# A graph network's opening: x ahead of the convolution taps, in block order, planned, with zero matmuls ahead of it

## The chip, the cores and the metric

The kernel runs on one NeuronCore of a Trainium2 chip. Five engines work at once and are tied by semaphores: TensorE (PE, matmuls into PSUM), VectorE (DVE), ScalarE (ACT), GpSimd (POOL) and SyncE (SP), which here only issues DMA transfers. The metric is the time on the device in microseconds (us), the median of several executions.

## The reference

Input: `x` of shape (64, 256, 256), that is 64 graphs of 256 nodes with 256 channels, and an adjacency matrix of 256 x 256 for each graph. One layer is computed, all in float32:

```
h     = relu(layernorm(x))                    # no learned scale
c     = relu(bn1(conv1(h)))                   # conv of width 1 over the nodes, 256 to 256 channels
x_conv= relu(bn2(conv2(c)) + h)               # conv of 17 taps over the nodes, 256 to 256 channels
s     = h @ w_se.T + b_se                     # 3 numbers for each node
A     = exp(-|s_n - s_m|^2) * adj
x_nmp = A @ relu(h @ w_msg.T + b_msg)
out   = x + GRU(input=[x_conv, x_nmp], state=h)   # sigmoid r and z, tanh n
```

## The kernel before

**Tiling.** The graphs are taken in pairs (`G = 2`, 32 pairs), and eight graphs (four pairs, `PB = 4`) make a block; there are eight blocks. The convolution of 17 taps is done in a transformed domain: the nodes of a graph are seen as `(b h c)` with 16 blocks b, 8 positions h and 2 halves c, so that 16 nodes make a block of length `L = 16`; additions on VectorE (`split`, then `forward` with an odd and an even part) transform the blocks, TensorE multiplies each of 16 frequencies by its filter (`begin`, `complete`), and `branch_back` and the like transform back.

**Filters.** The transformed filters are made once, in the opening. `filter_steps` calls `filters` 57 times (19 groups of input channels by three passes over the frequencies): two matmuls of the taps by fixed points, a copy from PSUM by ScalarE into one of the buffers `evicted`, and a DMA write of that buffer to a DRAM tensor `filt`. From there `load_kinds` brings filters back into nine slots `wb`, 256 KB each, for the products.

**The opening.** Loads are issued first (from `nc.first = 0` to `nc.first = None`, line 685 on), in this order for each queue: the vectors of the second batch norm by GpSimd; fixed points, half of the first taps, the vectors of the first batch norm, the conv1 weights and the other taps by ScalarE; and by SyncE the other half of the first taps, x of pair 0, more taps, x of pair 1, more taps, x of pairs 2 and 3. Then for each pair of the first block: `norm` (statistics on VectorE, a power of -1/2 on GpSimd, scaling on VectorE), `transpose_h` (eight transposes by TensorE into PSUM, evicted with the relu into `HT`), `conv1` (matmuls; evicted with scale, shift and relu into `h1`) and `split`. Evictions of pair 0 are done by VectorE, the others by ScalarE. Filter steps are put between the pairs. After that come `forward(0)`, which needs pairs 0 and 1, `forward(1)`, which needs pairs 2 and 3, the remaining filter steps, and `message`, `embed` and `affinity` of pair 0.

**Rows of x.** `rows` gives the DMA side of a graph as `(b h c) d -> h b (c d)`: the partition is h x 16 + b, and each holds two rows, 2 KB, in a row. `transpose_h` can then write `HT` in the order of PSUM, which is the order `(c, h, b)` that the rest of the kernel uses.

**The order of the work.** No instruction is issued at once: `Recorder` keeps every operation with the operations it depends on, and `emit` writes them out. `plan` is a list scheduler: it has a cost for each operation, and for a DMA a size in us (from the bytes, the length of runs and `share`, a number of parallel parts) and one common clock `self.dma`; at each step it takes the engine that can start first and on it the operation whose due time `late` (counted back from TensorE's program order) is least. Operations recorded while `nc.first` is a number keep their order ahead of all others. With `emit(True)` the order is that of the code, and only the times are kept. The kernel has three such parts: the four pairs of the opening with `emit(True)`, `forward` up to the last filter step with `emit()`, and the main loop over the eight blocks with `emit()`.

All operations are recorded through one helper line, so the profile shows line L370 nearly everywhere, and the names of tiles tell the work apart: `aux` and `acc` are PSUM buffers, `fo` the filter evictions, `x`, `T`, `Sv`, `PT` the places of pairs 0 to 3 (the last three are unused halves of other buffers), `st`, `mv`, `rstd` the statistics, `U`, `V`, `Sv`, `T`, `PT` the transforms.

Of the kernel before, what the change touches and what calls it, by code (L numbers as in the profile page):

```python
# [13 lines left out]
FP = mybir.dt.float32  # L14
U16 = mybir.dt.uint16
AF = mybir.ActivationFunctionType
ALU = mybir.AluOpType
# [232 lines left out]
class Recorder:  # L250
# [14 lines left out]

    def __init__(self, nc):
        self.nc, self.tasks, self.live, self.masks = nc, [], {}, {}
        self.first, self.planned, self.dma = None, 0, 3.0
        self.lanes = [deque([0.0] * self.LANES) for _ in range(2)]
        self.free = dict.fromkeys(self.LAG, 0.0)  # L270
        for name in ("tensor", "vector", "scalar", "gpsimd", "sync"):
            setattr(self, name, Proxy(self, name))
# [60 lines left out]
    def record(self, engine, op, args, kw):  # L333
        method = getattr(getattr(self.nc, engine), op)
        out = kw["out"] if "out" in kw else args[0]
        ins = [v for v in list(args) + list(kw.values()) if isinstance(v, bass.AP) and v is not out]
        n = 1
        for s in out.shape[1:]:
            n *= s
        size = 0  # L340
        if op.startswith("dma"):
            if "transpose" in op:
                size, cost = 2.5, self.TURN
            elif "accum_op" in kw:
                size, cost = 2.3, 1.0
            else:
                k = 10 if engine == "gpsimd" else self.share(out, ins[0])
                run = min(self.run(v) for v in (out, ins[0]))
                size = n * out.shape[0] * WIDTH[out.dtype] * 16 / k / 330e3 * max(1, 1400 / run)
                cost = 0.35 if k > 10 and run > 1024 else 0.62  # L350
        elif engine == "tensor":
            cost = n / 597 + 0.006
            if op == "transpose":
                cost = out.shape[-1] / 1170
            elif args[1].shape[0] < 32:
                cost = 0.23
        elif engine == "vector":
            cost = {"bn_stats": 0.33, "bn_aggr": 0.07}.get(op, n / 960 + 0.07)
            if op == "tensor_mul" and n == 256:
                cost = 0.5  # L360
        elif engine == "scalar":
            cost = n / 1400 + (0.2 if op == "activation" else 0.12)
            if out.dtype == U16:
                cost = n / 860
            elif len(out.shape) == 3 and op == "activation" and n == 256:
                cost = 0.49
        else:
            cost = 1.1 if self.planned == 0 else 7.0 if ALU.pow in args else 2.0
        k = len(self.tasks)
        self.tasks.append(Task(engine, lambda: method(*args, **kw), cost, size, self.first))  # L370
        if self.first is not None:
            self.first += 1
        for v in ins:
            self.access(k, v, False)
        self.access(k, out, True)
        return k
# [106 lines left out]
def kernel(  # L483
# [19 lines left out]
    P = 128  # L503
# [33 lines left out]
    def keep(name, *dims):  # L537
        return const.tile([P, *dims], FP, name=name)
# [24 lines left out]
    st, mv, rstd, shift = (Ring(keep(f"{name}{k}", *dims) for k in range(2)) for name, dims in (  # L563
        ("st", (G * MC, 6)), ("mv", (G * MC, 2)), ("rstd", (G * MC,)), ("shift", (G * MC,))))
    SLOTS = 9
    slots = [keep(f"wb{k}", DC, D) for k in range(SLOTS)]
    aux = Ring(psum.tile([P, W], FP, name=f"aux{k}") for k in range(4))
    acc = Ring(psum.tile([P, 2, W], FP, name=f"acc{k}") for k in range(2))
# [12 lines left out]
    def rows(t, g):  # L581
        return t[g].rearrange("(b h c) d -> h b (c d)", h=L // 2, c=MC)

    def row_tile(t, g):
        return t[:, g * MC:(g + 1) * MC, :].rearrange("p c d -> p (c d)")
# [5 lines left out]
    def chunk(t, g, c):  # L591
        return t[:, g * N + c * P:g * N + (c + 1) * P]
# [2 lines left out]
    SPARE = {k + 1: t[:, SL // 4:] for k, t in enumerate((Tt, Svt, PTt))}  # L595
    X, ADJ, HT, XNM, STATS = {}, {}, {}, {}, {}

    def load_rows(t, src, i, eng):
        for g in range(G):
            eng.dma_start(out=row_tile(t, g), in_=rows(src, G * i + g))  # L600

    def load_x(i, eng=nc.sync):
        if i >= NP:
            return
        X[i] = SPARE[i].rearrange("p (q d) -> p q d", d=D) if i in SPARE else x_rows
        load_rows(X[i], x, i, eng)

# [38 lines left out]

    PASSES = [range(0, 6), range(6, 12), range(12, 16)]
    taps = stage.tile([KG * TAPS, NG, DC, D], FP, name="taps")  # L650
    evicted = Ring(stage.tile([P, W], FP, name=f"fo{k}") for k in range(6))
    bank_points = [filter_points(p, TAPS) for p in PASSES]
    points = [stage.tile([P, KG * f.shape[1]], FP, name=f"points{n}") for n, f in enumerate(bank_points)]

    def load_taps(dc, a, b, eng):
        v = c2_wT[dc * P + a * KG:dc * P + b * KG].rearrange("(g k) t o -> (k t) g o", k=KG)
        eng.dma_start(out=taps[:MAIN, a:b, dc, :], in_=v[:MAIN])
# [9 lines left out]
    def load_points(n, eng):  # L667
        f = bank_points[n]
        m = np.zeros((P, KG, f.shape[1]), np.float32)
        for k in range(KG):  # L670
            m[k * TAPS:(k + 1) * TAPS, k] = f
        eng.dma_start(out=points[n], in_=tc.nc.inline_tensor(m.reshape(P, -1), name=f"points{n}").ap())
# [4 lines left out]
    def load_vectors(name, srcs, eng):  # L677
        n = [v.shape[0] // P for v in srcs]
        t = const.tile([sum(n), P], FP, name=f"{name}_rows")
        for j, v in enumerate(srcs):  # L680
            a = sum(n[:j])
            eng.dma_start(out=t[a:a + n[j]], in_=v.rearrange("(k p) -> k p", p=P))
        ROWS[name] = t, n

    nc.first = 0
    load_vectors("bn2", bn2 + [ih_b, hh_b], nc.gpsimd)
    load_points(0, nc.scalar)
    for dc, eng in ((0, nc.sync), (1, nc.scalar)):
        load_taps(dc, *PARTS[0], eng)
        load_last_taps(dc, eng)  # L690
    load_x(0)
    load_vectors("bn1", bn1, nc.scalar)
    nc.scalar.dma_start(out=w_c1, in_=c1_wT.rearrange("(k p) o -> p k o", p=P))
    for n in range(1, len(PASSES)):
        load_points(n, nc.scalar)
    load_taps(0, *PARTS[1], nc.sync)
    load_x(1)
    load_taps(1, *PARTS[1], nc.scalar)
    load_taps(0, *PARTS[2], nc.sync)
    load_taps(1, *PARTS[2], nc.scalar)  # L700
    load_last_group(0, nc.sync)
    load_last_group(1, nc.scalar)
    load_x(2)
    load_x(3)
    nc.first = None
    nc.gpsimd.memset(Z, 0.0)
    nc.gpsimd.memset(Z[:, 0, :, 2 * SE:KD], 1.0)
# [2 lines left out]
    nc.scalar.activation(keep("unused", 1), neg_half[:, :1], AF.Relu)  # L710

    mm, transpose = nc.tensor.matmul, (lambda p, v: nc.tensor.transpose(p, v, ident))

    def columns(name):
        t, n = ROWS[name]
# [24 lines left out]
    def norm(i):  # L740
        stats(i)
        for j in range(G * MC):
            nc.vector.tensor_scalar(X[i][:, j, :], X[i][:, j, :], STATS[i][1][:, j, 0:1], STATS[i][2][:, j:j + 1],
                                    ALU.subtract, ALU.mult)
# [14 lines left out]
    def transpose_h(i):  # L759
        HT[i] = hts()  # L760
        for dc in range(DC):
            p = aux()
            for j in range(G * MC):
                transpose(chunk(p, j // MC, j % MC), X[i][:, j, dc * P:(dc + 1) * P])
            if i == 0:
                nc.vector.tensor_scalar(HT[i][:, dc, :], p, 0.0, None, ALU.max)
            else:
                nc.scalar.activation(HT[i][:, dc, :], p, AF.Relu)

# [421 lines left out]
    def filter_steps(n):  # L1193
        for _ in range(n):
            banks[0] += 1
            p = acc()[:, 0] if banks[0] % 3 == 0 else aux()
            filters(p, *steps.popleft(), nc.gpsimd if len(steps) % 2 else nc.sync)
# [1 line left out]
    norm(0)  # L1199
    bn1 = columns("bn1")  # L1200
    s1, h1_shift = fold_bn(bn1, "bn1")
    filter_steps(2)
    transpose_h(0)
    norm(1)
    for j in range(PB):
        if j > 0:
            transpose_h(j)
        if 0 < j < PB - 1:
            norm(j + 1)
        if j == 2:  # L1210
            nc.gpsimd.dma_start(out=w_msg[:, :, D:], in_=se_wT.rearrange("(k p) s -> p k s", p=P))
            for t, v in ((b_msg[:, :D], msg_b), (b_msg[:, D:], se_b)):
                nc.gpsimd.dma_start(out=t, in_=bass.AP(tensor=v.tensor, offset=v.offset, ap=[[0, P], [1, v.shape[0]]]))
            nc.sync.dma_start(out=w_msg[:, :, :D], in_=msg_wT.rearrange("(k p) o -> p k o", p=P))
            load_adj(0, nc.sync)
        conv1(j, True)
        if j == 2:
            *bn2, b_ih, b_hh = columns("bn2")
            s2, h2_shift = fold_bn(bn2, "bn2", 1.0 / L)
            b_rz = keep("b_rz", 2 * DC)  # L1220
            nc.vector.tensor_add(b_rz, b_ih[:, :2 * DC], b_hh[:, :2 * DC])
            nc.vector.tensor_scalar(b_rz, b_rz, 0.5, None, ALU.mult)
        split(j)
        filter_steps((4, 6, 2, 2)[j])
    nc.emit(True)
    load_x(PB)
    forward(0)
    forward(1)
# [201 lines left out]
```

## Time and profile before

| | |
|---|---|
| time, median of 3 | 1750.55 us (1741.92 to 1751.39) |
| span of the profiled execution | 1740.1 us |
| TensorE busy | 1667.2 us, 96% |
| VectorE busy | 1463.1 us, 84% |
| ScalarE busy | 1039.5 us, 60% |
| GpSimd busy | 245.6 us, 14% |
| DMA | 260.88 MB, mean 150 GB/s |

In the trace the opening lasts to about 110.6 us, when the last filter matmul ends and the first product of the main loop starts; it is 6% of the span. The rows of digits in the page are tenths of busy time in 40 equal slices, each 43.5 us here. A table by stretch gives, for each engine, the busy time and the number of instructions in parentheses. "MATMUL ... x8" counts machine instructions: a float32 matmul of the code appears as two of them, a transpose as one. The chain lists what was waited for, with start and length in us.

### The profile page before, as it was taken

How to read it: one execution, taken by the hardware profiler on the slowest of the kernel's cores; microseconds unless marked ns; L12 is line 12 of the kernel's file. 1: busy time of each engine (PE TensorE's matmuls, PEld its weight loads, DVE VectorE, ACT ScalarE, POOL GpSimd, SP SyncE). 2: the span in 40 equal slices, each digit the busy share in tenths (PEclk: the TensorE clock that was granted, in tenths of full speed). 3: DMA queues.
4: the chain of work that ended last, by engine and by line, in shares of the span. 5: the costliest groups of instructions: out<-in, count | busy, mean ns of one | idle time of the engine just before them, and what ended most of it. 6: DMA issues, size and time to landing. Idle time of an engine off the chain costs nothing.

```text
span 1740.1 us, 26075 instructions
## 1 busy us (share of the span) xinstructions
PE 1667.2 (96%) x8950; PEld 1414.8 (81%) x8950; DVE 1463.1 (84%) x3400; ACT 1039.5 (60%) x1949; POOL 245.6 (14%) x241
## 2 busy tenths in 40 slices
PE   5989999999999999999999999999999999999996
PEld 3768788888789888897888887898888978888885
DVE  3888998799897998788987988979988889879553
ACT  1545665576656756567655766557566666556543
POOL 2210231002210221102211031102211022100010
PEclk9999999999999999999999999999999999999998
DMA  8775365875669565684657746595656846375122
GB/s 192 224 263 176 73 140 116 244 190 105 124 130 281 118 137 112 169 244 98 127 121 231 189 98 117 127 275 122 137 106 185 234 97 126 75 234 135 22 52 49
DMA packets 326264, 260.88 MB, mean 150 GB/s; under 512 B 204616, under 2 KB 252004, under 8 KB 326131
## 3 DMA queue, kind: packets, MB, share of 16 engines
q1 hardware_dynamic: 293738, 213.72, 46.5%
q0 software_dynamic: 29440, 42.83, 12.9%
q10 hardware_dynamic: 2953, 2.66, 0.8%
q8 instruction: 70, 1.15, 0.3%
q14 instruction: 63, 0.52, 0.1%
HBM read 156.03 MB, written 43.78 MB: 115 GB/s over the span
## 4 chain that ended last, share of the span: by engine, by line
PE 84%; DVE 7%; DMA 6%; ACT 2%; issue 1%; SPq 0%; POOL 0%; ACTq 0%; DVEq 0%
PE acc L370 58%; PE aux L370 26%; DMA wb<-filt 3%; DVE V L370 2%; DVE T L370 1%; DMA x<-in_x_dram 1%; DMA hh<-halves 1%; DMA T<-in_x_dram 1%; DVE U L370 1%; DVE tr L370 1%; DVE acc L370 0%; SPq L370 0%; DVE e L370 0%; DVE gn L370 0%; ACT e L370 0%
## 5 line engine op out<-in xcount | busy, mean ns | idle before, releaser
L370 PE MATMUL acc<-wb,w_ih 128*128 128x256 f32 x768 | 192.4, 379 | 0.0
L370 POOL DMA_DIRECT2D back<-in_x_dram x62 | 63.0, 1154 | 763.3 <-ACT back L370 738.7
L370 PEld LDWEIGHTS acc<-wb,w_ih 128*128 128x128 f32 x768 | 145.9, 190 | 19.8
L370 POOL TENSOR_TENSOR rstd<-rstd,neg_half 128x4 f32<-128x4 f32 x32 | 88.6, 2768 | 418.9 <-DVE shift L370 214.7
L370 PE MATMUL acc<-wb,w_x 128*128 128x256 f32 x576 | 137.3, 382 | 8.6 <-DVE acc L370 8.6
L370 PE MATMUL aux<-wb,w_x 128*128 128x256 f32 x576 | 140.0, 381 | 3.6 <-ACT e L370 2.8
L370 DVE SCALAR_TENSOR_TENSOR V<-T,V 128x128 f32<-128x128 f32 (+2 forms) x448 | 141.1, 382 | 0.0
L370 PEld LDWEIGHTS acc<-wb,w_x 128*128 128x128 f32 x576 | 107.7, 190 | 36.3 <-DVE acc L370 16.3
L370 PEld LDWEIGHTS aux<-wb,w_x 128*128 128x128 f32 x576 | 107.7, 190 | 22.1 <-ACT e L370 5.2
L370 PE MATMUL acc<-V,wb 128*128 128x128 f32 x1024 | 118.7, 276 | 4.9 <-DMA wb<-filt 3.6
L370 PE MATMUL aux<-w_msg,hT 128*128 128x259 f32 x512 | 121.5, 382 | 0.4 <-ACT fo L370 0.4
L370 PEld LDWEIGHTS acc<-V,wb 128*128 128x128 f32 x1024 | 116.2, 192 | 6.1 <-DMA wb<-filt 4.6
L370 PEld LDWEIGHTS acc<-U,wb 128*128 128x128 f32 x1024 | 116.9, 192 | 0.9
L370 PE MATMUL acc<-U,wb 128*128 128x128 f32 x1024 | 117.1, 275 | 0.0
L370 DVE TENSOR_TENSOR T<-Yv 128x512 f32<-128x512 f32 (+1 forms) x80 | 42.5, 581 | 85.6 <-ACT Yv L370 85.1
L370 ACT COPY back<-gn 128x1024 uint16<-128x1024 uint16 x62 | 81.3, 1348 | 49.7 <-DMA gn<-back 49.7
L370 PE MATMUL aux<-hT,w_c 128*128 128x512 f32 x224 | 107.1, 596 | 3.8 <-ACT e L370 2.7
L370 PE MATMUL acc<-wb,w_hh 128*128 128x256 f32 x384 | 109.9, 381 | 0.0
L370 PE MATMUL acc<-Yv,w_ih 128*128 128x256 f32 x384 | 109.6, 381 | 0.1
L370 PEld LDWEIGHTS aux<-w_msg,hT 128*128 128x128 f32 x512 | 96.3, 190 | 15.4 <-ACT fo L370 0.8
L370 PE MATMUL acc<-hT,w_hh 128*128 128x256 f32 x384 | 105.6, 381 | 0.7 <-ACT acc L370 0.7
L370 PE MATMUL acc<-xnm,w_ih 128*128 128x256 f32 x384 | 103.9, 379 | 0.0
(176 smaller groups left out, 3841.0 us busy)
## 6 DMA issues: line engine op xcount, KB each, us to landing
wb<-filt SPq DMA_DIRECT2D x376, 256.0 KB
back<-in_x_dram POOLq DMA_DIRECT2D x62, 256.0 KB, 7.4
out_dram<-back POOLq DMA_DIRECT2D x62, 256.0 KB, 4.3
x<-in_x_dram SPq DMA_DIRECT2D x58, 256.0 KB
halves_d<-halves SPq DMA_DIRECT2D x28, 512.0 KB
adjh<-halves_d SPq DMA_DIRECT2D x112, 128.0 KB
hh<-halves SPq DMA_DIRECT2D x108, 128.0 KB
filt<-fo POOLq DMA_DIRECT2D x18, 252.0 KB, 5.1
```

Source lines behind the costliest of these rows:

```text
L370: self.tasks.append(Task(engine, lambda: method(*args, **kw), cost, size, self.first))
```

## The change

It concerns the opening only, and has five parts.

1. x of the first four pairs is loaded ahead of all taps (on SyncE's queue), and the vectors of the first batch norm move to GpSimd's queue, so that the pairs can be worked on while the taps come in.
2. These loads, and that of pair 4 (`i <= PB`), take the rows in block order: `blocks` gives `(b h c) d -> b h (c d)`, one contiguous stretch of DRAM. The node order that the rest needs is restored in `transpose_h`: the eviction reads PSUM as `(q b h)` and writes `(q h b)`.
3. `emit(True)` is gone: the opening is planned together with `forward` and the filters. The steps put between the pairs are 1, 2, 3, 3 instead of 2 and then 4, 6, 2, 2. The planner's start of the DMA clock goes from 3.0 to 2.3, and the share of a GpSimd transfer becomes the larger of 10 and what the shapes give.
4. TensorE multiplies zeros 24 times (`WARM`) into a PSUM buffer that is overwritten later, from a tile that GpSimd sets to zero first, so that it has been at work when x comes.
5. Filter evictions have 8 buffers instead of 6. The second batch norm's folding and the loads of the message weights and the first adjacency move behind the fourth pair in the code.

```diff
-        self.first, self.planned, self.dma = None, 0, 3.0
+        self.first, self.planned, self.dma = None, 0, 2.3
...
-                k = 10 if engine == "gpsimd" else self.share(out, ins[0])
+                k = max(self.share(out, ins[0]), 10 if engine == "gpsimd" else 1)
...
+    WARM = 24
...
-    def load_rows(t, src, i, eng):
+    def load_rows(t, src, i, eng, rows=rows):
...
+    def blocks(t, g):
+        return t[g].rearrange("(b h c) d -> b h (c d)", h=L // 2, c=MC)
...
-        load_rows(X[i], x, i, eng)
+        load_rows(X[i], x, i, eng, blocks if i <= PB else rows)
...
-    evicted = Ring(stage.tile([P, W], FP, name=f"fo{k}") for k in range(6))
+    evicted = Ring(stage.tile([P, W], FP, name=f"fo{k}") for k in range(8))
...
     nc.first = 0
+    nc.gpsimd.memset(e_tile[:, 0], 0.0)
+    load_vectors("bn1", bn1, nc.gpsimd)
     load_vectors("bn2", bn2 + [ih_b, hh_b], nc.gpsimd)
+    nc.scalar.dma_start(out=w_c1, in_=c1_wT.rearrange("(k p) o -> p k o", p=P))
+    for j in range(PB):
+        load_x(j)
     load_points(0, nc.scalar)
     for dc, eng in ((0, nc.sync), (1, nc.scalar)):
         load_taps(dc, *PARTS[0], eng)
         load_last_taps(dc, eng)
-    load_x(0)
-    load_vectors("bn1", bn1, nc.scalar)
-    nc.scalar.dma_start(out=w_c1, in_=c1_wT.rearrange("(k p) o -> p k o", p=P))
...
-    load_taps(0, *PARTS[1], nc.sync)
-    load_x(1)
...
-    load_x(2)
-    load_x(3)
...
+    p = aux()
+    for _ in range(WARM):
+        mm(p[:, :P], e_tile[:, 0, 0, :P], e_tile[:, 0, 0, :P], start=True, stop=True)
...
+            t = HT[i][:, dc, :].rearrange("p (q h b) -> p q h b", h=L // 2, b=NW)
+            u = p.rearrange("p (q b h) -> p q h b", h=L // 2, b=NW)
...
-                nc.vector.tensor_scalar(HT[i][:, dc, :], p, 0.0, None, ALU.max)
+                nc.vector.tensor_scalar(t, u, 0.0, None, ALU.max)
...
-    filter_steps(2)
-    transpose_h(0)
-    norm(1)
     for j in range(PB):
         if j > 0:
-            transpose_h(j)
-        if 0 < j < PB - 1:
-            norm(j + 1)
...
+            norm(j)
+        transpose_h(j)
         conv1(j, True)
...
         split(j)
-        filter_steps((4, 6, 2, 2)[j])
-    nc.emit(True)
+        filter_steps((1, 2, 3, 3)[j])
```

More of the change, by code (lines that the diff above doesn't have):

```diff
@@ L690 @@
         load_last_taps(dc, eng)
-    load_x(0)
-    load_vectors("bn1", bn1, nc.scalar)
-    nc.scalar.dma_start(out=w_c1, in_=c1_wT.rearrange("(k p) o -> p k o", p=P))
     for n in range(1, len(PASSES)):
         load_points(n, nc.scalar)
-    load_taps(0, *PARTS[1], nc.sync)
-    load_x(1)
-    load_taps(1, *PARTS[1], nc.scalar)
-    load_taps(0, *PARTS[2], nc.sync)
-    load_taps(1, *PARTS[2], nc.scalar)
+    for part in PARTS[1:]:
+        load_taps(0, *part, nc.sync)
+        load_taps(1, *part, nc.scalar)
     load_last_group(0, nc.sync)
     load_last_group(1, nc.scalar)
-    load_x(2)
-    load_x(3)
     nc.first = None
@@ L764, in transpose_h @@
                 transpose(chunk(p, j // MC, j % MC), X[i][:, j, dc * P:(dc + 1) * P])
+            t = HT[i][:, dc, :].rearrange("p (q h b) -> p q h b", h=L // 2, b=NW)
+            u = p.rearrange("p (q b h) -> p q h b", h=L // 2, b=NW)
             if i == 0:
-                nc.vector.tensor_scalar(HT[i][:, dc, :], p, 0.0, None, ALU.max)
+                nc.vector.tensor_scalar(t, u, 0.0, None, ALU.max)
             else:
-                nc.scalar.activation(HT[i][:, dc, :], p, AF.Relu)
+                nc.scalar.activation(t, u, AF.Relu)
     HP = P // 2
@@ L1201 @@
     s1, h1_shift = fold_bn(bn1, "bn1")
-    filter_steps(2)
-    transpose_h(0)
-    norm(1)
     for j in range(PB):
         if j > 0:
-            transpose_h(j)
-        if 0 < j < PB - 1:
-            norm(j + 1)
[L1210 to L1215, printed above, removed]
-        conv1(j, True)
[L1217 to L1222, printed above, removed]
-        split(j)
-        filter_steps((4, 6, 2, 2)[j])
-    nc.emit(True)
+            norm(j)
+        transpose_h(j)
+        conv1(j, True)
+        split(j)
+        filter_steps((1, 2, 3, 3)[j])
+    *bn2, b_ih, b_hh = columns("bn2")
+    s2, h2_shift = fold_bn(bn2, "bn2", 1.0 / L)
+    b_rz = keep("b_rz", 2 * DC)
+    nc.vector.tensor_add(b_rz, b_ih[:, :2 * DC], b_hh[:, :2 * DC])
+    nc.vector.tensor_scalar(b_rz, b_rz, 0.5, None, ALU.mult)
+    nc.gpsimd.dma_start(out=w_msg[:, :, D:], in_=se_wT.rearrange("(k p) s -> p k s", p=P))
+    for t, v in ((b_msg[:, :D], msg_b), (b_msg[:, D:], se_b)):
+        nc.gpsimd.dma_start(out=t, in_=bass.AP(tensor=v.tensor, offset=v.offset, ap=[[0, P], [1, v.shape[0]]]))
+    nc.sync.dma_start(out=w_msg[:, :, :D], in_=msg_wT.rearrange("(k p) o -> p k o", p=P))
+    load_adj(0, nc.sync)
     load_x(PB)
```

## The prediction

> **What bounds the kernel now.** I read first the engine rows of the page, then a table of engine time by stretch of the opening, then the chain of waits through it, and last the order of instructions on TensorE. The page:
>
> ```profile
> PE   5989999999999999999999999999999999999996
> ...
> PEclk9999999999999999999999999999999999999998
> ...
> PE 84%; DVE 7%; DMA 6%; ACT 2%; issue 1%; SPq 0%; POOL 0%; ACTq 0%; DVEq 0%
> ```
>
> TensorE is the bound: full in nearly every slice, 84% of the chain. The first slice (43.5 us) is the one with a hole. The stretches (columns: PE, PE weight load, DVE, ACT and POOL busy, PE clock, DMA share, GB/s):
>
> ```profile
> 0.00:16.00 16.00, 0.00 (x0) 0.00 (x0) 0.75 (x2) 0.00 (x0) 5.50 (x17) 1.00 0.77 143
> 16.00:40.00 24.00, 19.41 (x55) 12.11 (x56) 14.07 (x45) 5.98 (x10) 4.48 (x6) 0.86 0.93 234
> 40.00:60.00 20.00, 19.32 (x78) 12.49 (x77) 11.26 (x39) 11.02 (x19) 6.89 (x10) 1.00 0.52 163
> 60.00:80.00 20.00, 20.00 (x93) 16.52 (x92) 20.00 (x51) 11.67 (x22) 5.33 (x10) 1.00 0.81 251
> 80.00:110.60 30.60, 25.82 (x108) 16.11 (x106) 29.93 (x88) 16.59 (x42) 6.58 (x12) 0.89 0.71 218
> 110.60:140.00 29.40, 26.25 (x214) 25.27 (x214) 18.06 (x52) 8.04 (x15) 3.10 (x4) 1.00 0.93 325
> ```
>
> TensorE does nothing for 16 us, VectorE is half idle until 60, and both are then full to 110.6, where the last filter matmuls end and the products of the main loop begin. The chain says why:
>
> ```profile
> 2.48 13.67 DMA x<-in_x_dram
> ...
> 16.17 10.65 DMA T<-in_x_dram
> ...
> 113.06 8.05 PE acc L370 x72
> ...
> 121.13 10.75 DMA wb<-filt
> ```
>
> The start is two loads of x in a row: pair 0 complete at 16.2, pair 1 (into tile T) at 26.8. The DMA rate in the first of them shows that the loads are slow, not only late:
>
> ```profile
> 2.80:5.60 2.80, 0.00 (x0) 0.00 (x0) 0.00 (x0) 0.00 (x0) 2.74 (x8) 1.00 1.15 227
> 5.60:11.20 5.60, 0.00 (x0) 0.00 (x0) 0.00 (x0) 0.00 (x0) 0.70 (x1) 1.00 0.79 108
> ```
>
> 227 GB/s while the first taps move, 108 once x and the last tap rows are what is left. The same filter matmuls also differ:
>
> ```profile
> 16.28 3.93 PE L370 MATMUL aux<-taps,points 119*126 119x256 f32 x8
> 40.87 1.89 PE L370 MATMUL aux<-taps,points 119*126 119x256 f32 x8
> ```
>
> Right after the idle stretch the same eight take twice as long.
>
> [...]
>
> **The change, part by part.**
>
> *Work on TensorE.* None of the opening's real work is removed. 57 filter steps: four instructions take 0.86 us in the chain, so 49.0 us. conv1: 3.70 us per pair in the timeline, 14.8 for four. Transposes: 1.04 per pair, 4.2. Messages: 16 instructions, 0.86 per four, 3.5. Embedding, affinity, transposes of e and vectors: about 3.5. Sum 75 us, against 94.5 us from 16.1 to 110.6. So 19.5 us of that stretch are waits and slow clock, on top of 16 empty ones.
>
> *x first, in block order.* First data moved at 2.8 us. Pair 0 is 0.51 MB, and ScalarE's queue (conv1 weights, points) moves some 0.35 MB beside it: 0.86 MB at 227 GB/s is 3.8 us, so pair 0 is there at 6.6 (at 350 GB/s, the best slice of these 16 us, 5.3). I take 6.6, against 16.2. All four pairs and what runs beside them, 2.9 MB at 230 GB/s, are there by about 15.4. SyncE's half of the first taps, 0.47 MB, follows at 17.5. Filter steps thus start 1.2 us *later* than now; this is the price of the new order.
>
> *Vectors of bn1* now go by the GpSimd queue, where such loads took 9.2 to 9.9 us to land: ready at 11 to 13. The first to need them is the eviction of conv1 of pair 0, at about 15. Nothing.
>
> *TensorE until 17.5.* Norm of pair 0: statistics 1.5, aggregation 0.36, one add, the power on GpSimd about 1.2 with its hand-over, scaling 1.38: 4.5 us. Transposes start at 11. By 17.5 TensorE has done about one pair, 4.7 us of the 75.
>
> *Then.* 17.5 + 70.3 = 87.8 if it never waits. In the present trace TensorE and its weight loads still wait on ACT evictions, e and messages for about 5 us between 84 and 110; I keep 4 of them. The last filter step ends at about **92**, instead of 110.6.
>
> *VectorE.* It was busy 82.4 us from 13.9 to 117.2, of which 1.9 belong to pair 4: 80.5. From 6.6, with 5 us of holes at the start, it ends at 92 as well. The even half of the second forward (8 us of it, 105.5 to 115.3, less 1.6 for e) is not needed for the first products, so VectorE does not hold up the main loop. It leaves no room for more, though.
>
> *DMA.* From the stretches: 2.3 + 5.6 + 3.3 + 5.0 + 6.7 = 22.9 MB up to 110.6. In 89 us that is 257 GB/s; 251 was moved at a share of 0.81, and 298 at 0.99 (80 to 90). It fits, barely.
>
> *Planned opening.* The list scheduler, with its 1.1 us for GpSimd operations and 330 GB/s for DMA, now sets the order from the start; before, it was the order of the code. This is what lets the first forward transform begin after pair 1 and not after pair 3 (62.1). I count it in the 92, not separately. The two more eviction buffers take away some of the 7.1 us for which ScalarE waited on filter writes; in the 92 too.
>
> *Zero matmuls.* 24 calls are 48 instructions of 128 columns: 0.114 each at speed (64 in 7.31 us)[...]: 5.5 to 11 us from about 1.5. They end between 7 and 12.5; real work comes at 11. Between nothing and 1.5 us, and the slow clock (2.0 us in the first eight filter matmuls) is saved. I take zero for the cost. The memset before them: 0.5 us by the h memset (1152 elements, 1.05 us), hidden in the load.
>
> *Strided reads of PSUM in the transposes' eviction.* Nothing at best. At worst as e times adj, which reads with a stride: 587 ns against 405 for a plain product of that size, so +45%, or 0.27 us on 0.60. Ten evictions, eight on ScalarE (busy 60%): hidden; 0.6 us on VectorE at worst.
>
> *Sum.* The main loop starts 110.6 − 92 = 18.6 us sooner. It is in essence the same code, and TensorE-bound, so the shift carries to the end: 1750.55 − 18.6 = **1732**.
>
> **Rivals.**
>
> *Evictions and writes become the bound.* For it: 257 GB/s is needed throughout, and 3.3 MB of taps still load while filter writes begin; at one step per 0.86 us these alone ask for 293 GB/s (252 KB each). Against it: 60 to 80 ran at full TensorE with 0.81 share. If 22.9 MB move at the 234 GB/s of 16 to 40, the end is at 2.8 + 98 = 101: gain 9.6, **1741**.
>
> *Everything overlaps.* Loads at 350 GB/s (pair 0 at 5.3, taps at 12.5) and no waits left: 12.5 + 70.3 = 83 to 85, gain 26, **1724**. Against it: VectorE's 80.5 us from 5.3 leave it no hole at all.
>
> *The load is hidden anyway.* Later filter steps push the same work back, and the wait for wb (10.75 us at 121) grows by what is won: **1750**. Against it: that wait comes with a DMA share of 0.93 in the main loop's own loads, which move with it.
>
> *Slower.* The main loop is planned from another starting state (DMA backlog, queue lanes), and 1.6 ms of order can come out differently. TensorE is idle 73 us in the span, 26 of it before 110.6. If a new order adds 60% of the other 47, 28 us, against the 18.6: 1750.55 − 18.6 + 28 = **1760**. For it: the planner's DMA constant and the share of GpSimd transfers change too. Against it: the loop's code, queues and buffers are the same, and a shift of the start leaves relative times alone.
>
> **How the numbers follow.** Forecast 55%, evictions 20%, everything overlaps 10%, hidden 5%, slower 10%. The range goes from 1719 (everything overlaps, and 5 us for a luckier plan) to 1748 (evictions, and the spread of the time before, 1741.92 to 1751.39, on it); it leaves out the last two cases. Faster by over 0.5% means under 1741.8: all of the forecast but a few in a hundred, everything overlaps, and half of evictions: 0.76. Within 0.5%: the rest of evictions, hidden, a little of the others: 0.14. Slower 0.10.
>
> **What would show it.** Right: x complete at 6 to 7 us in the chain; real transposes at about 11; filters from 17 to 18; the first products on Sv at about 92; eight filter matmuls in 1.9 us from the start; the stretch from there to the end as long as now (1629 us). Wrong: a long wait of ScalarE for filter writes or TensorE for taps between 15 and 40 (evictions); products at 92 but a longer rest (replanning); zero matmuls on the chain after pair 0 has been scaled.

## The result, and the profile after

The changed kernel takes 1735.81 us (median of 7 runs, 1732.92 to 1745.35) against 1747.11 us for the kernel before (7 runs, 1740.95 to 1753.16). The ratio is 0.994, 95% interval 0.9911 to 0.9969: faster by about 0.6%, some 11 us where 18.6 were forecast. With all further runs that were taken beside the experiments below, the medians are 1748.0 us (111 runs of the kernel before) and 1735.5 us (24 runs of the changed one, these seven among them), a gain of 12.5 us. In the profiled executions the span falls from 1740.1 to 1733.1 us.

The lines of the page that answer to those of before:

```profile
PE   8999999999999999999999999999999999999996
...
PEclk9999999999999999999999999999999999999998
...
PE 87%; DMA 5%; DVE 5%; ACT 2%; issue 1%; SPq 0%; POOL 0%; ACTq 0%; DVEq 0%; POOLq 0%
```

The hole in the first slice is closed (8 instead of 5, part of it zeros), and TensorE's share of the chain rises from 84% to 87%. The stretches, with the same columns as before:

```profile
0.00:16.00 16.00, 11.60 (x60) 9.79 (x61) 8.26 (x35) 1.49 (x2) 10.84 (x25) 0.91 0.96 225
16.00:40.00 24.00, 24.00 (x92) 14.39 (x91) 21.12 (x50) 11.21 (x21) 3.78 (x6) 0.99 0.93 231
40.00:60.00 20.00, 20.00 (x92) 16.20 (x92) 20.00 (x71) 12.64 (x23) 8.73 (x15) 1.00 0.85 234
60.00:80.00 20.00, 18.80 (x87) 14.50 (x86) 19.38 (x53) 10.38 (x25) 4.78 (x9) 1.00 0.90 290
80.00:110.60 30.60, 28.11 (x160) 21.26 (x159) 14.45 (x49) 13.81 (x31) 6.50 (x10) 0.89 0.82 287
```

VectorE is now nearly full from 16 us (21.1 of 24, before 14.1), and the DMA rate in the first 16 us is 225 GB/s instead of 143. The order on TensorE shows the steps of the opening:

```profile
1.85 7.80 PE L370 MATMUL aux<-e 128*128 128x128 f32 x48 [1.85 <-POOL e L370]
11.51 0.33 PE L370 MATMUL aux<-ident,x 128*128 128x128 f32 x1 [1.87 <-DVE x L370]
...
13.61 5.21 PE L370 MATMUL acc<-hT,w_c 128*128 128x512 f32 x8 [0.69 <-DVE hT L370]
...
18.98 1.03 PE L370 MATMUL aux<-taps,points 119*126 119x256 f32 x4
...
94.02 2.51 PE L370 MATMUL acc<-Sv,wb 128*128 128x128 f32 x16
```

Zeros to 9.65, real transposes from 11.5, filters from 19.0, and the first product of the main loop (`acc<-Sv,wb`) at 94.0. Before, it stood at 110.6. So the opening won 16.6 us in this pair of executions, and the span only 7.0: from the first product to the end it took 1629.5 us before and 1639.1 after. Where did the 9.6 us go?

The table gives the start of the first product of each block. The gap to the kernel before shrinks by a little in most blocks:

| block | 0 | 1 | 2 | 3 | 4 | 5 | 6 | 7 | end |
|---|---|---|---|---|---|---|---|---|---|
| before, us | 110.6 | 321.0 | 523.6 | 725.4 | 931.0 | 1132.5 | 1333.6 | 1537.6 | 1740.1 |
| after, us | 94.0 | 306.3 | 511.3 | 713.5 | 918.6 | 1122.7 | 1325.5 | 1528.0 | 1733.1 |
| gap | 16.6 | 14.7 | 12.3 | 11.9 | 12.4 | 9.8 | 8.1 | 9.6 | 7.0 |

The written order of the two programs differs only in block 0 and at the start of block 1; from there on every engine has the same instructions in the same order. What differs is TensorE's clock. In the kernel after, at the starts of blocks 3, 4, 5 and 6 (the clock is the third number from the end):

```profile
713.00:716.40 3.40, 2.92 (x14) 2.96 (x15) 3.40 (x7) 1.04 (x3) 0.00 (x0) 0.50 0.74 276
917.80:924.60 6.80, 5.98 (x28) 6.01 (x29) 4.90 (x9) 1.12 (x2) 0.00 (x0) 0.50 0.55 187
1122.60:1126.00 3.40, 3.31 (x15) 3.35 (x16) 3.40 (x7) 0.72 (x1) 0.00 (x0) 0.50 0.65 237
1327.40:1330.80 3.40, 2.94 (x14) 2.94 (x14) 3.40 (x7) 1.00 (x2) 0.00 (x0) 0.50 0.68 255
```

Two more lie inside blocks, at 317.1 and 1593.6. The kernel before has only two such stretches after its first product, at 724.7 and 1335.7 (in both kernels the last microseconds of the run, also at half clock, are left out); at the start of its block 4 it waits as well and keeps its clock. First block 4 of the kernel after, then blocks 3 and 4 of the kernel before:

```profile
918.62 6.67 PE L370 MATMUL acc<-Sv,wb 128*128 128x128 f32 x32 [3.05 <-DMA wb<-filt]
```

```profile
725.43 6.71 PE L370 MATMUL acc<-Sv,wb 128*128 128x128 f32 x32 [2.53 <-DMA wb<-filt]
930.96 3.81 PE L370 MATMUL acc<-Sv,wb 128*128 128x128 f32 x32 [2.53 <-DMA wb<-filt]
```

The bracket is TensorE's idle time ahead of the products, until the block's first filters are loaded. After 3.05 us the same 32 instructions take 6.67 us instead of 3.81; after 2.53 us they take 6.71 in one block of the kernel before and 3.81 in the next.

This pair of executions is not a typical one. Only 4 of the 111 further runs of the kernel before were as fast as the one profiled (1741.92 us); its granted clock was 0.990 on average, that of the profiled execution after 0.986. Over the runs themselves the mean clock is practically the same, 0.9876 before (111 runs) and 0.9881 after (24 runs). So the clock can account for the 9.6 us of this pair (27.3 us at half clock after the first product, against 10.2 in the kernel before), but not, in general, for what the changed kernel gains less than its opening does.

### The profile page after: what moved, and what is told of

Read it like the earlier page. It is cut to its first block, busy times and chain, and to the rows that moved or that the text cites. A ratio compares the mean times of both kernels' runs of the same rounds, so it can differ in the third digit from the quotient of the medians.

```text
span 1733.1 us, 26180 instructions
## 1 busy us (share of the span) xinstructions
PE 1678.7 (97%) x8998; PEld 1427.0 (82%) x8998; DVE 1461.7 (84%) x3400; ACT 1038.5 (60%) x1949; POOL 254.6 (15%) x246
## 4 chain that ended last, share of the span: by engine, by line
PE 87%; DMA 5%; DVE 5%; ACT 2%; issue 1%; SPq 0%; POOL 0%; ACTq 0%; DVEq 0%; POOLq 0%
PE acc L370 60%; PE aux L370 27%; DMA wb<-filt 2%; DVE V L370 1%; DMA filt<-fo 1%; DVE T L370 1%; DMA hh<-halves 1%; DMA T<-in_x_dram 0%; ACT e L370 0%; DVE acc L370 0%; DVE tr L370 0%; DVE e L370 0%; DVE gn L370 0%; DMA x<-in_x_dram 0%; ACT back L370 0%
## 5 line engine op out<-in xcount | busy, mean ns | idle before, releaser
L370 POOL TENSOR_TENSOR rstd<-rstd,neg_half 128x4 f32<-128x4 f32 x32 | 96.0, 2999 | 390.6 <-DVE shift L370 225.4
L370 PEld LDWEIGHTS aux<-w_msg,hT 128*128 128x128 f32 x512 | 96.3, 190 | 16.1 <-ACT fo L370 1.6
```

## The experiments

Two theories about the 9.6 us. **A**: the opening is worth what it shows at the first product, and part is lost because TensorE falls to half clock after the waits of 2 to 3 us at the starts of blocks, in some executions and not in others. **B**: the main loop lost time because it was planned anew.

**Filled, first try.** Both kernels (the result of the extra matmuls is not used), with work for TensorE in the wait:

```diff
+    FILL = 12
...
+    def fill(n):
+        last = max(k for k, t in enumerate(nc.tasks) if t.engine == "tensor")
+        p = aux()
+        for _ in range(n):
+            nc.tasks[mm(p[:, :P], ident, ident, start=True, stop=True)].preds.add(last)
...
+        if b > 0:
+            fill(FILL)
         begin(0)
```

> The changed kernel, plus 12 TensorE instructions pairs on the identity matrix (result unused) ahead of the first product of blocks 1 to 7, so that TensorE works through the wait at the block's start. Theory A (the 16.6 us won by the opening are partly given back because TensorE falls to half clock after those 2 to 3 us waits[...]): the half-clock stretches at block starts go from five to none or one, the first 32 products of a block take 3.8 us everywhere, the time falls 6 to 10 us below the changed kernel, ratio to before 0.987 to 0.991, and the spread between runs shrinks. Theory B (the main loop lost time because it was planned anew): no gain, the ratio stays at 0.994 or gets worse by up to 7 x 2.7 us.

> The kernel before with the same 12 instruction pairs ahead of the first product of blocks 1 to 7. Theory A: the kernel before loses its own half-clock stretches, two or three in a run: ratio 0.995 to 0.999, and the changed kernel with them is 15 to 17 us faster than this one, the whole gain of the opening. Theory B: no gain, ratio 1.000 to 1.010; the difference to the other filled kernel stays at 7 to 11 us.

Measured: ratios 1.000 (0.9983 to 1.0016) and 1.0026 (1.0015 to 1.0037). The half-clock stretches at the starts of blocks 3 to 6 are gone in both (these blocks took 202 to 204 us), but the times got worse. The planner had put the extra work into its order: it moved the affinity matmuls and took a buffer of the ring, and block 0, where nothing is filled, went from 212.3 to 220.6 us in the changed kernel. A's numbers are missed; B's ratios came true, though not its 7 to 11 us between the two filled kernels (3.4). Neither is tested by this, since the order changed too.

**The main loop in the old order.** The changed kernel, its main loop written out by a list of the order that the kernel before has:

```diff
-    nc.emit()
+    nc.emit_as(ORDER)
```

> The changed kernel with its main loop written out in exactly the order that the kernel before has (only block 0 and the start of block 1 differ in the changed kernel). Theory A: block 0 gets back 2 us at most, the half-clock stretches remain a matter of chance: ratio 0.992 to 0.995. Theory B: the rest after the first product is as long as before, 1629 us, ratio 0.990 to 0.991.

Measured: 0.9917 (0.9891 to 0.9942), an interval that holds both expectations. The profiled execution, a single one, speaks against B: with the old order the rest after the first product is 1638.0 us, not 1629, and its half-clock stretches sum to 23.9 us. The same opening ended at 99.0 here, not at 94.0.

**Parts of the opening.** The block order undone:

```diff
-        load_rows(X[i], x, i, eng, blocks if i <= PB else rows)
+        load_rows(X[i], x, i, eng)
...
-            t = HT[i][:, dc, :].rearrange("p (q h b) -> p q h b", h=L // 2, b=NW)
-            u = p.rearrange("p (q b h) -> p q h b", h=L // 2, b=NW)
+            t, u = HT[i][:, dc, :], p
```

> The changed kernel with x of the first five pairs in the old row order (and a plain eviction of the transposes). If the block order matters[...]: pair 0 complete at 8 to 10 us instead of 5.1, pair 3 at 25 instead of 16, first product of the main loop at 97 to 100 instead of 94.0. Rival, the loads are hidden behind TensorE's filters anyway: first product at 94 to 95.

Measured: 0.9956 (0.9941 to 0.9971). The second half of pair 0 is there at 8.5 us instead of 5.1, and the first product comes at 106.6, later than expected. TensorE in the opening with the old row order:

```profile
12.96 1.41 PE L370 MATMUL aux<-ident,x 128*128 128x128 f32 x8 [2.60 <-DVE x L370]
...
27.18 1.96 PE L370 MATMUL aux<-taps,points 119*126 119x256 f32 x8 [1.74 <-DMA taps<-in_c_wT_dram]
...
43.75 0.23 PE L370 MATMUL aux<-ident,bn_rows 20*128 20x20 f32 x1
...
78.04 1.22 PE L370 MATMUL aux<-taps,points 119*126 119x256 f32 x2 [4.06 <-DVE msg L370]
```

Transposes come 1.5 us later than in the changed kernel and filters 8.2 us later. SyncE's taps stand behind x on the same queue, and with the slower x TensorE waits for taps until 27.2 us; in the profiled execution of the changed kernel it uses them from 19.0, without a wait. That is not the loss, though: the plan puts conv1 of pair 1 ahead of the filters, and TensorE waits 1.74 us for the taps. Where both kernels have done the same work, at the transpose of `bn_rows`, this one is 4.1 us behind (43.75 against 39.63). The rest of the 12.6 us comes later: 4.06 us in which TensorE waits until VectorE has added the bias to messages, and 20.1 us at half clock up to the first product instead of 9.0.

Zeros taken out:

```diff
-    WARM = 24
+    WARM = 0
```

> The changed kernel without the 24 multiplications of zeros. If they keep the clock up for the first real work: the first eight transposes and conv1 of pair 0 take longer without them, and the first product of the main loop comes 1 to 3 us later than 94.0. Rival, they end 1.9 us before x is ready and the clock falls anyway (conv1 of pair 0 took 5.2 us with them, 3.7 in other pairs): no change, 93.5 to 94.5.

Measured: 0.9954 (0.9922 to 0.9985), 1736.76 us, first product at 96.9. Executions of the changed opening lie between 93.9 and 99.0 (below), so no effect can be seen. conv1 of pair 0 runs slowly with the zeros too (5.21 us against 3.70); without them it took 5.79 us, and with them 5.15 to 6.54 in six executions of the changed opening.

Planning alone, that is the kernel before with one line less:

```diff
         filter_steps((4, 6, 2, 2)[j])
-    nc.emit(True)
```

And the loads alone, that is the kernel before with the new order of loads, the block order with its eviction, and the first batch norm's vectors on GpSimd:

```diff
+    load_vectors("bn1", bn1, nc.gpsimd)
     load_vectors("bn2", bn2 + [ih_b, hh_b], nc.gpsimd)
+    nc.scalar.dma_start(out=w_c1, in_=c1_wT.rearrange("(k p) o -> p k o", p=P))
+    for j in range(PB):
+        load_x(j)
     load_points(0, nc.scalar)
...
-        load_rows(X[i], x, i, eng)
+        load_rows(X[i], x, i, eng, blocks if i <= PB else rows)
```

> The kernel before with one line taken out: the opening is planned together with the forward transforms and filters, and the loads stay as they were. If planning is the larger part of the 16.6 us: first product at 100 to 103 instead of 110.6. If the loads are: at 106 to 110, since x of pair 0 still comes at 14 to 16 us.

> The kernel before with x loaded ahead of all taps and in block order, and the first batch norm's vectors on GpSimd's queue; order of the code in the opening, no zeros, six eviction buffers. If the loads are the larger part: first product at 98 to 102. If planning is: at 105 to 109. If the two need each other (VectorE must have x early and be free to start the first transform early), this one and the planned one together give less than 16.6 us.

Measured: planning alone is *slower*, 1.0127 (1.0092 to 1.0163), first product at 127.0, 16.5 us later than before; neither expectation had that. The loads alone win 5.2 us at the first product (105.4, within the range for planning as the larger part) and 0.9989 (0.9979 to 0.9999) in time. That the two need each other is the expectation that held: their sum is far under 16.6 us. TensorE with planning alone:

```profile
12.44 1.19 PE L370 MATMUL aux<-taps,points 119*126 119x256 f32 x2 [2.96 <-DMA taps<-in_c_wT_dram]
...
25.66 2.07 PE L370 MATMUL aux<-taps,points 119*126 119x256 f32 x4 [3.26 <-DMA points<-points]
...
32.36 1.41 PE L370 MATMUL aux<-ident,x 128*128 128x128 f32 x6
...
60.09 2.25 PE L370 MATMUL aux<-ident,Sv 128*128 128x128 f32 x8 [10.42 <-issue]
```

The planner lets taps come first and early (it counts 330 GB/s; 141 were moved in these 16 us), so it writes filter steps ahead of the transposes. On the chip taps and points land later, TensorE stands at them in its order, and x, scaled at 24.9, waits until 32.4. The longest wait, 10.42 us, comes at the transposes of pair 2 (tile `Sv`): VectorE begins that pair's statistics at 53.5, behind parts of the first transform. That it stands so late in the plan because of the wrong transfer times is likely, but not shown.

The loads alone have the opposite fault. The order of the code, made for taps that come first, has two filter steps ahead of the transposes of pair 0. TensorE waits for the taps although pair 0 is scaled by 12.8:

```profile
19.88 3.75 PE L370 MATMUL aux<-taps,points 119*126 119x256 f32 x8 [7.55 <-DMA taps<-in_c_wT_dram]
23.42 1.76 PE L370 MATMUL aux<-ident,x 128*128 128x128 f32 x8
```

So an order and the loads that it was made for belong together: 5.2 us and −16.5 alone, 16.6 for all parts of the change together in the profiled pair. Whether the planner is needed for this was not tested: the new loads with an order written by hand for them, transposes first, may do as well. Nor were the planner's two constants and the new spread of the steps (1, 2, 3, 3) changed alone.

Six eviction buffers instead of eight:

```diff
-    evicted = Ring(stage.tile([P, W], FP, name=f"fo{k}") for k in range(8))
+    evicted = Ring(stage.tile([P, W], FP, name=f"fo{k}") for k in range(6))
```

> The changed kernel with 6 filter eviction buffers instead of 8. If the number of buffers holds back the filters between 50 and 68 us, where ScalarE waits for filter writes: the first product moves from 94.0 to 96 or later (it was 94.0, 93.9 and 99.0 in three executions of the same opening). If the rate of the writes does: 94 to 95, and the time is that of the changed kernel, ratio to before 0.992 to 0.996.

Measured: 0.9927 (0.99 to 0.9953), 1737.82 us, first product at 99.5: at the end of the range of the unaltered opening. Between 43 and 100 us TensorE waits five times for ScalarE's filter evictions, 5.2 us in all; with eight buffers it waited once in each of six executions, 1.2 to 3.3 us. The buffers thus do what they are for, but what they are worth in time stays open.

**Filled in place.** Ten pairs of instructions, eight in block 6, are put in when the order is written out, after planning, so that nothing else moves. They write where the next affinity matmul writes (the lines that make and record them are left out here):

```diff
         for k in self.plan(fixed):
+            if k in self.ahead:
+                self.ahead[k]()
             self.tasks[k].call()
```

> The changed kernel in exactly its own order on every engine, with 10 pairs of TensorE instructions on the identity matrix (8 in block 6) ahead of the affinity matmuls that stand before the first product of blocks 3 to 6, where TensorE has nothing to do for 2 to 3 us. Their result is overwritten unused. Theory A (half-clock stretches after those waits give back part of the gain): none of them is left at the start of blocks 3 to 6, and since nothing else moves, the rest after the first product falls from 1639 to 1628 to 1633, ratio to before 0.988 to 0.992. Rival: the extra instructions cost what they save, as in the first filled kernel, where blocks 2 to 6 took 202.4 to 203.6: ratio 0.993 to 0.997.

> The kernel before in exactly its own order, with the same instructions at the same places. Theory A: its own half-clock stretches at those places vanish too, ratio 0.995 to 0.998, and the changed kernel filled the same way is 12 to 16 us faster. Rival: 1.000 to 1.003.

Measured: 0.9906 (0.9883 to 0.9929), 1731.34 us, for the changed kernel; 0.998 (0.997 to 0.9991), 1744.83 us, for the kernel before. Block 4 of the changed kernel, filled:

```profile
915.33 2.39 PE L1002 MATMUL aux<-ident 128*128 128x128 f32 x20
917.66 0.71 PE L371 MATMUL aux<-zT 9*128 9x256 f32 x8
918.69 3.81 PE L371 MATMUL acc<-Sv,wb 128*128 128x128 f32 x32 [0.32 <-DMA wb<-filt]
```

```profile
918.70:922.50 3.80, 3.80 (x34) 3.80 (x35) 3.69 (x7) 2.67 (x7) 0.00 (x0) 1.00 0.80 268
```

The products start no earlier than without, but the clock is full and they take 3.81 us. No half-clock stretch is left at the starts of blocks 3 to 6, in either kernel. In the changed kernel the rest after the first product is 1630.4 us (expected 1628 to 1633). The difference between the two filled kernels is 13.5 us of the medians, within the 12 to 16 of theory A.

**Once more**, with no edit, the changed kernel and the filled one on the same chip:

> The changed kernel once more, beside the filled one on the same chip. Theory A: first product between 94 and 99, half-clock time after it between 10 and 30 us and the rest after the first product 1624 us plus half of that time; ratio to before 0.992 to 0.996. Rival (the profiled execution was an odd one): the rest after the first product does not follow the half-clock time.

> The changed kernel filled in place once more, beside the changed kernel on the same chip. Theory A: 3 to 6 us faster than the changed kernel, ratio to before 0.988 to 0.992, and again no half-clock stretch at the start of blocks 3 to 6. Rival: no difference between the two beyond their intervals.

Measured: 0.9936 (0.9921 to 0.9952), 1735.13 us, and 0.9927 (0.9899 to 0.9955), 1734.54 us. For the changed kernel theory A's numbers hold: first product at 96.7, 17.1 us at half clock, which give 1624 + 8.5 = 1632.5 us for the rest, and 1633.7 were measured. For the filled one they are missed (0.6 us faster, not 3 to 6). The filled kernel again has no half-clock stretch at those places, but the two times can't be told apart here. The filling removes what it was meant to remove; that it makes the changed kernel faster is not shown. For the kernel before it is, by 0.2%. What all runs show, though not all were taken side by side, is the clock itself: a mean of 0.9905 in 12 runs of the filled kernel against 0.9881 in 24 of the changed one, and 0.9904 in 22 filled runs of the kernel before against 0.9876 in 111.

**All profiled executions together.** For each kernel without filling: the time from the first product to the end, and the sum of half-clock stretches in it (those that begin after it, without the last one, at the end of the run):

| kernel | first product, us | half clock, us | rest, us |
|---|---|---|---|
| before | 110.6 | 10.2 | 1629.5 |
| row order | 106.6 | 13.7 | 1632.0 |
| no zeros | 96.9 | 17.1 | 1632.8 |
| loads only | 105.4 | 17.1 | 1634.5 |
| changed, again | 96.7 | 17.1 | 1633.7 |
| six buffers | 99.5 | 23.9 | 1636.5 |
| old main order | 99.0 | 23.9 | 1638.0 |
| changed | 94.0 | 27.3 | 1639.1 |
| planning only | 127.0 | 30.7 | 1640.6 |

A line fitted to them (1624.4 us plus 0.53 times the half-clock time) misses none by more than 1.1 us. Half a microsecond for each microsecond at a clock of 0.50 is also my estimate for a TensorE that has work all the time: in the kernel before, eight transposes at 0.50 (from 34.36 us) took 1.91 us, and eight at 1.00 (from 46.05) took 1.04. The order of the main loop, old or new, makes no difference of more than 1 us on this line. The three executions filled in place, which were not used for the fit, took 1630.4, 1629.0 and 1633.1 us with 10.2, 6.8 and 10.2 us at half clock: the line misses the first two by 1 us or less and the last by 3.3, so something other than the clock can cost that much too.

## Why the prediction was right, and where it was off

The time came out near the forecast, by the mechanism forecast: x is there early, TensorE begins early, and the main loop starts earlier. But the gain is two thirds of the 18.6 us at most (11.3 us in the seven runs each, 12.5 in all), and it lies nearer to the 9.6 of the rival of evictions. That 1735.8 is only 4 us from 1732 is in part luck: 1732 was counted from 1750.55, the median of three runs; from 1747.11 it would have been 1728.5.

*x first, in block order.* Right: pair 0 complete at 5.1 us (forecast 6.6), and at 8.5 with the row order. Why the block order lands sooner was not shown. I had the price for the taps as 1.2 us; filters began at 19.0 instead of 16.3. But TensorE was at conv1 of pair 0 until 18.8 and did not wait for taps; in two of the five other executions of this opening it did, for 0.55 and 1.07 us.

*Vectors of bn1: nothing.* True of the profiled execution. In two of the six executions listed below, TensorE waited 1.6 us for these vectors in the midst of the first transposes.

*TensorE until 17.5.* Transposes at 11.5 (forecast 11; 10.4 to 12.2 in those six). VectorE, in its order, waited for pair 1's load before it scaled pair 0. One pair was done later than at 17.5: filters begin at 20.4 on average.

*Then: the last filter step at 92.* The right mechanism, mis-sized terms. Six executions of this opening (the changed kernel, three times filled, once more, and with the old main order) have the first product at 94.0, 93.9, 97.5, 96.5, 96.7 and 99.0, mean 96.3; the opening of before ended at 110.6, 111.0 and 110.1. So the opening wins 14.3 us on average, not 18.6. Of the 4.3 us that are missing, 2.9 are lost before the filters begin (20.4 instead of 17.5), and 1.4 after that (75.9 us instead of the 74.5 that hold 4 us of waits). In the slower executions TensorE waits longer for ScalarE, which waits for filter writes (2.4 to 3.3 us, against 1.2 and 1.8 in the two at 94), and in three of these four it falls to half clock at about 71 to 73 us (with the old main order, after 2.68 us without work, four message matmuls took 2.09 us there, against 1.14 in the changed kernel): a part of the rival of evictions.

*VectorE and DMA.* Right: VectorE's even half of the second transform ends at 91.1 (forecast 92), 290 GB/s are moved at a share of 0.90 between 60 and 80.

*Planned opening: counted in the 92, not separately.* Wrong as a thought: alone it costs 16.5 us. It is worth something only with loads that its order fits.

*Zero matmuls: saving 2.0 us of slow clock.* Not found, and this is the largest part of the 2.9 us. The 2.0 us were 3.93 us for eight filter matmuls after the idle start less 1.89 for eight later ones; the clock reads 1.00 at both places, so that a slow clock made the difference was my estimate. So was the upper end of 11 us for the zeros, twice their 5.5 as 3.93 is twice 1.89; they took 7.80. The zeros end 1.9 us before the first transpose; half clock then falls on conv1 of pair 0 (0.50 from 13.3 to 16.7 us), which takes 5.15 to 6.54 us, on average 2.1 more than the 3.70 that I counted, and without the zeros no loss can be measured.

*Strided reads of PSUM.* The two evictions of a pair by ScalarE take 1.09 us as a group, 1.08 before: the lower bound, nothing.

*The shift carries to the end.* In the profiled pair it did not: "the stretch from there to the end as long as now (1629 us)" became 1639.1 us. The reason was not my rival of a new plan but the clock, by 17.1 more us at half of it, about 9 us. That is a matter of the execution: the changed kernel, executed again, had 17.1 us of it and a rest of 1633.7, and the 1629 came from one of the fastest runs of the kernel before. Over all runs the step nearly holds: 12.5 us between the medians, 14.3 at the first product, with the mean clock equal. The 14.3 rests on six and three executions that differ by 5 and 1 us, so the 2 us between them may be nothing. Block 0 is a candidate (210.4 and 211.4 us with the opening of before, 212.3, 213.4, 212.8 and 215.1 with the new one); which part is clock and which is waiting for filters stays open.

## What to carry to other kernels

A plan is worth what its assumptions on transfers are worth: planning an opening whose loads come later than the planner thinks put the wrong work at the head of TensorE's order (waits of 2.96 and 3.26 us for taps and points, while x, scaled at 24.9, stood until 32.4) and cost 16.5 us, and the same planner with early, quick loads won. New loads in an old order lose most of their worth in the same way (5.2 us). Give the first load the shape in which it lands soonest (5.1 against 8.5 us here); the taps behind it on its queue were there sooner too (in use at 19.0 us, against a wait until 27.2). And before a difference of half a per cent is put down to code, compare the clock records, and those of many runs: here the sum of half-clock stretches accounts for the length of the main loop to within 1.1 us in nine profiled executions, while the mean clock over all runs was the same before and after. One profile each would have shown 7 us where the medians show 11 to 12.

## What the runs showed of the hardware that was not expected

TensorE was at half clock after idle times of 1.96 us (block 5, for 3.4 us) and of 3.05 us (block 4, for 6.8 us) in the kernel after. It kept its clock after 2.53 us in block 4 of the kernel before, but lost it after the same 2.53 us in that kernel's block 3: one wait, both outcomes. With work whose result nobody reads in such a wait (20 instructions, 2.39 us, in blocks 3 to 5; 16, 1.95 us, in block 6) it kept it in every one of three executions filled in place. After the zeros and a gap of 1.87 us the transposes of pair 0 took 273 ns each, against 421 without the zeros; but conv1, after a second gap of 0.69 us, took 5.21 us instead of 3.70, with half clock from 13.3 to 16.7 us. And a clock of 1.00 was no proof of speed at the start of a run: in the kernel before it reads 1.00 from 16 to 20 us, while the first eight filter matmuls take 3.93 us instead of the 1.89 that eight take from 40.87.
